# Row-by-row fetching on SyncE and ScalarE in a recommendation kernel: 245 tiles against 386

## The chip, the cores and the metric

The kernel runs on one core of one Trainium2 chip. Its time is the device time of one execution in microseconds. The kernel before took 10938.21 us (median of three runs, 10936.02 to 10938.97).

## The reference

For each of 16,384 samples, 69 user fields and one label index a table of 100,001 rows of 96 floats (384 bytes a row). An attention network gives each gathered row a weight, the weighted rows are summed by groups of fields, and a small top network follows:

```python
u = emb[batch_user]                              # 16384 x 69 x 96
q = emb[batch_label[:, 0]] broadcast over fields
z = concatenate([q, u, q - u, q * u])
h = dice(z @ W1 + b1, a1)                        # 64 wide
att = (h @ W2 + b2) @ W3 + b3                    # one weight per row
pre = where(batch_user < ITEM_NUM, u * att, 0)
pooled = einsum('gf,bfe->bge', window, pre)      # 69 fields into 10 groups
x = concatenate([pooled, ql])
h = dice(bn(x @ Wf1 + bf1), af1); h = dice(bn(h @ Wf2 + bf2), af2)
return h @ Wf3 + bf3
```

`dice(x)` is `(alpha * (1 - p) + p) * x` with `p = sigmoid(x)` after a constant scale. The arithmetic is float32.

## The kernel before, in words

The samples are cut into 32 blocks of 512. A block has 69 chunks of 512 rows each: 64 that mix eight samples with 64 fields, and 5 for the tail fields. Two chunks make a pair, and there are 1104 pairs; one **step** of the kernel is the work on one pair. A chunk is four tiles of 128 rows, so that a pair has eight tiles of 128 gathered rows.

A tile of rows comes to SBUF in one of three ways.

- Nearly all are gathered by GpSimd (POOL): one indirect DMA of 128 rows per tile (`gather`, L265, called from `fetch`, L373) into one slot of the tile `u` of the pool `upool`.
- SyncE (SP) fetches 109 tiles row by row. It issues one DMA of 384 bytes per row (L301), with the row's address taken from a register; every 32 rows it loads 32 offsets from SBUF into registers (L286).
- ScalarE (ACT) fetches 136 tiles in the same way, 16 rows in each step, between its own activations.

Tiles that SP and ACT fetch take slot 3 of a chunk and go to buffers of their own, the `ring`: four for SP and three for ACT. TensorE waits for the row count of such a tile on a semaphore (`wait_for_single`, L318) before it transposes it.

The order of the work on every engine is written out by hand: `plan` (L592) lists for each step what is recorded, and each engine runs its own instructions in that order. In step i these are, in order, the row sums of a group of four pairs (`attend_rows`, `spread`, every fourth step), `hidden(i - 2)` (four matmuls into `ph`, then two activations on ACT, L405 and L406, and a multiplication on VectorE, L407), ACT's rows of this step (`scalar_rows`, L615), `pool(i - 7)` (16 matmuls that read `u` or the ring a second time, and a copy to `pooled`), and `fetch(i)` (eight gathers or waits, eight transposes into two `ptr` tiles in PSUM, and two VectorE operations on each). What reads a tile `u` last is thus the pooling seven steps later; `upool` has 14 buffers. For each block some steps hold more: copies of a small table by ACT (`head_rows`, L342, two copies in one step), and the top network (L487 to L522) spread over ten steps, with six activations on ACT.

SP's list is short: the loads of indices and its rows. It runs ahead of the other engines until a ring buffer is not free yet.

Of the kernel before, what the change touches and what calls it, by code (L numbers as in the profile page):

```python
# [18 lines left out]
P = 128  # L19
# [29 lines left out]

ROW_BYTES = 4 * E  # L50
SLOT = 3
SP_CHUNKS = [2 * (10 * s + 8) + 1 for s in range(109)]
SP_RING = 4
ACT_CHUNKS = [2 * (8 * s + 11) for s in range(136)]
ACT_RING = 3
ACT_ROWS = 16
ACT_STEPS = -(-P // ACT_ROWS)
SINGLES = SP_CHUNKS + ACT_CHUNKS
NSB = (len(SINGLES) + P - 1) // P
NSEM = 8  # L60


def chunk_of(c):
# [52 lines left out]
def rec_kernel(  # L116
# [12 lines left out]
    nc = tc.nc  # L129
# [1 line left out]

    const = ctx.enter_context(tc.tile_pool(name="const", bufs=1))
    ipool = ctx.enter_context(tc.tile_pool(name="ipool", bufs=2))
    upool = ctx.enter_context(tc.tile_pool(name="upool", bufs=14))
    tpool = ctx.enter_context(tc.tile_pool(name="tpool", bufs=4))
    ypool = ctx.enter_context(tc.tile_pool(name="ypool", bufs=6))
    rpool = ctx.enter_context(tc.tile_pool(name="rpool", bufs=2))
# [137 lines left out]
    class Singles:  # L275

        def __init__(self, name, engine, kind, chunks, first, buffers, group):
            self.name, self.engine, self.kind, self.group = name, engine, kind, group
            self.chunks, self.first, self.buffers = chunks, first, buffers
            self.sems = [tc.alloc_semaphore(f"{name}{k}") for k in range(NSEM)]  # L280
            self.given = [0] * NSEM

# [12 lines left out]
        def fetch(self, s, start, stop):  # L295

            b, k = self.buffers[s % len(self.buffers)], s % NSEM
            for r in range(start, stop):
# [295 lines left out]
    def at(step, *work):  # L594
        plan.setdefault(step, []).extend(work)

    by_sync = Singles("sp", nc.sync, mybir.EngineType.SP, SP_CHUNKS, 0, range(SP_RING), 32)
    for s, m in enumerate(SP_CHUNKS):
        at(max(0, m // 2 - 6), lambda s=s: by_sync.fetch(s, 0, P))

    by_scalar = Singles(
        "act",
        nc.scalar,
        mybir.EngineType.Activation,
        ACT_CHUNKS,
        len(SP_CHUNKS),
        range(SP_RING, SP_RING + ACT_RING),
        2 * ACT_ROWS,
    )
    turn = {}  # L610
    for s, m in enumerate(ACT_CHUNKS):
        for k in range(ACT_STEPS):
            turn.setdefault(m // 2 - 2 - ACT_STEPS + k, []).append((s, k * ACT_ROWS, min(P, (k + 1) * ACT_ROWS)))

    def scalar_rows(i):  # L615

        for s, start, stop in turn.get(i, []):
            by_scalar.fetch(s, start, stop)

    c = NPAIR - CLOSE  # L620
    for i in range(c):
        if i >= 3 and (i - 3) % 4 == 3:
            at(i, rows_of(i - 6, 4))
        if i >= 3:
            at(i, tails_of(i - 3))
        if i >= 4 and (i - 4) % 4 == 3:
            at(i, spread_of(i - 7, 4))
        if i >= 2:
            at(i, hidden_of(i - 2))
        at(i, lambda i=i: scalar_rows(i))  # L630
        if i < c - CLOSE:
            if i >= POOL_LAG:
                at(i, pool_of(i - POOL_LAG))
        else:

            for k in {0: (-15, -14), 1: (-13,), 3: (-12, -11), 4: (-10, -9), 7: (-8, -7)}.get(i - c + 8, ()):
                at(i, pool_of(c + k))
        at(i, fetch_of(i))
# [116 lines left out]
```

## Time and profile before

| | |
|---|---|
| median of three runs | 10938.21 us |
| the profiled execution | 10926.71 us |
| its span, first to last instruction | 10924.9 us |
| mean granted TensorE clock | 0.745 |
| busy: PE / VectorE / ACT / POOL | 8862.0 / 4285.5 / 1897.5 / 8226.3 us |
| gathers on POOL, rows (L266) and labels | 8587 + 128 |
| single-row DMAs on ACT and on SP | 17408 and 13952 |
| busy share of the 16 DMA engines: gathers, ACT and SP rows | 18.7%, 0.5% and 0.4% |

All of these come from one profiled execution, except the median. The busy time of ACT does not hold its DMA issues or its register loads: they are instructions of its queue (written ACTq), and so are those of SP (SPq). An idle gap that the profile shows on ACT can therefore be filled with row issues. A wait "on issue" is time in which the engine waited for nothing that the profile shows.

### The profile page before, as it was taken

To read this page: it belongs to the slowest core of one execution; us is meant where nothing else is said; L and a number is where in the kernel's file an instruction comes from. 1 tells how busy PE (TensorE), PEld (TensorE's weight loads), DVE (VectorE), ACT (ScalarE), POOL (GpSimd) and SP (SyncE) were. 2 spreads that over 40 slices of the span, in tenths; PEclk is the share of its full clock that TensorE was granted. 3 is DMA by queue.
4 is the path that set the end of the run, shared out by engine and by line. 5 is a ranking of instruction groups with operands and counts; after the bars stand their busy time and mean duration, and the time that the engine had idled before them with its cause. 6 is when DMAs were issued, how large, how long until landed. Compare 5 with 4: busy or idle time off the path is not lost.

```text
span 10924.9 us, 172203 instructions
## 1 busy us (share of the span) xinstructions
PE 8862.0 (81%) x41797; PEld 4319.5 (40%) x41797; DVE 4285.5 (39%) x7535; ACT 1897.5 (17%) x2761; POOL 8226.3 (75%) x8721
## 2 busy tenths in 40 slices
PE   7878878788887888888878778878888887888878
PEld 3333434343333344333433333334343333433335
DVE  4334333333333333433333333333333333333334
ACT  1111111111111111111111111111111111111112
POOL 7777777777777777777777777777777777777776
PEclk7767777777777777767777777777777777777777
DMA  2212211121111212212111121112212112122111
GB/s 49 42 42 44 42 42 41 42 44 42 42 42 42 44 41 42 42 41 44 42 42 41 42 44 42 42 42 42 44 42 42 42 41 44 42 42 41 42 41 36
DMA packets 344467, 458.51 MB, mean 42 GB/s; under 512 B 202354, under 2 KB 202866, under 8 KB 343330
## 3 DMA queue, kind: packets, MB, share of 16 engines
q0 software_dynamic: 278880, 428.92, 18.7%
q1 hardware_dynamic: 29762, 11.82, 0.5%
q10 hardware_dynamic: 34816, 6.75, 0.4%
q8 instruction: 336, 5.51, 0.2%
q14 instruction: 673, 5.51, 0.2%
HBM read 446.74 MB, written 0.07 MB: 41 GB/s over the span
## 4 chain that ended last, share of the span: by engine, by line
POOL 49%; issue 21%; PE 17%; DMA 12%; DVE 0%; ACT 0%; ACTq 0%; POOLq 0%; DVEq 0%
POOL u L266 48%; DMA u<-in_rows,ids 12%; PE p L502 4%; PE acc L325 4%; PE ph L399 3%; PE ph L403 2%; PE ptr L325 2%; POOL q L266 1%; PE prow L414 1%; PE pa L423 1%; PE ph L396 0%; PE ph L401 0%; PE pc L348 0%; PE patt L431 0%; ACTq L301 0%
## 5 line engine op out<-in xcount | busy, mean ns | idle before, releaser
L266 POOL DMA_INDIRECT u<-in_rows,ids x8587 | 8104.3, 944 | 2620.1 <-issue 2428.2
L325 PE MATMUL ptr<-ident,u 128*96 128x128 f32 x8587 | 2002.8, 332 | 1940.1 <-DMA u<-in_rows,ids 1892.9
L407 DVE TENSOR_TENSOR y<-ph,y 128x512 f32<-128x512 f32 x1104 | 763.5, 692 | 4377.1 <-ACT y L406 4119.6
L325 PEld LDWEIGHTS ptr<-ident,u 128*96 128x96 f32 x8587 | 1139.7, 149 | 2701.4 <-DMA u<-in_rows,ids 2262.6
L325 PEld LDWEIGHTS acc<-rw,u 128*96 128x96 f32 x15930 | 1677.0, 187 | 1204.3 <-issue 977.6
L376 DVE COPY uT<-ptr 96x512 f32<-96x512 f32 x2208 | 1494.1, 677 | 1488.6 <-PE ptr L325 1485.2
L325 PE MATMUL acc<-rw,u 128*96 128x20 f32 x15930 | 1792.5, 258 | 57.8 <-DVE rw L436 41.7
L405 ACT ACTIVATE y<-ph 128x512 f32<-128x512 f32 x1104 | 658.6, 597 | 6308.6 <-PE ph L403 5822.7
L399 PE MATMUL ph<-uT,A 128*64 128x512 f32 x4096 | 1649.8, 883 | 0.0
L403 PE MATMUL ph<-quT,wn 96*64 96x512 f32 x4416 | 1585.2, 788 | 0.0
L379 DVE TENSOR_TENSOR quT<-ptr,qT 96x512 f32<-96x512 f32 x2048 | 1380.2, 674 | 0.0
L406 ACT ACTIVATE y<-y,wn,na1c 128x512 f32<-128x512 f32 x1104 | 898.1, 813 | 36.6
L403 PEld LDWEIGHTS ph<-quT,wn 96*64 96x64 f32 x4416 | 440.7, 188 | 1041.5 <-issue 1040.8
L502 PE MATMUL p<-pooled,wf 96*100 96x512 f32 (+1 forms) x1400 | 693.1, 644 | 0.0
L399 PEld LDWEIGHTS ph<-uT,A 128*64 128x64 f32 x4096 | 264.1, 175 | 616.2 <-issue 608.8
L416 ACT COPY row<-prow 128x512 f32<-128x512 f32 (+1 forms) x277 | 161.6, 583 | 1791.9 <-PE prow L414 1179.1
L470 DVE COPY pooled<-acc 96x160 f32<-96x160 f32 x1008 | 419.9, 417 | 117.6 <-PE acc L325 116.9
L414 PE MATMUL prow<-y,v 128*32 128x512 f32 x2208 | 453.6, 891 | 1.4 <-DVE y L407 1.1
L502 PE MATMUL p<-pre,V 96*100 96x512 f32 (+1 forms) x700 | 394.9, 710 | 3.0 <-DVE x L485 2.7
L502 PEld LDWEIGHTS p<-pooled,wf 96*100 96x100 f32 x1400 | 259.5, 198 | 332.6 <-issue 332.6
L436 DVE SCALAR_TENSOR_TENSOR rw<-patt,bb,wn 128x320 f32<-128x320 f32 x554 | 276.2, 539 | 143.6 <-PE patt L431 142.9
L431 PE MATMUL patt<-ident,row 128*128 128x128 f32 x1108 | 224.9, 340 | 25.1 <-DVE pre L424 22.7
(72 smaller groups left out, 2445.8 us busy)
## 6 DMA issues: line engine op xcount, KB each, us to landing
ring<-in_rows ACTq DMA_DIRECT2D x17408, 0.4 KB
ring<-in_rows SPq DMA_DIRECT2D x13952, 0.4 KB
u<-in_rows,ids POOLq DMA_INDIRECT x8587
ids<-in_idx SPq DMA_DIRECT2D x8, 560.0 KB, 3.9
q<-in_emb,ids POOLq DMA_INDIRECT x128
wf<-in_far SPq DMA_DIRECT2D x1, 1209.0 KB, 6.4
wn<-in_near SPq DMA_DIRECT2D x1, 236.0 KB, 2.8
ids<-in_idx SPq DMA_DIRECT2D x1, 140.0 KB, 2.3
```

The source lines that it names most:

```text
L266: nc.gpsimd.indirect_dma_start(out=dst, out_offset=None, in_=table, in_offset=bass.IndirectOffsetOnAxis(ap=index, axis=0),)
L325: ins = op(out, ring[:, at[0]].bitcast(F32) if at else u[:, 4 * (c % 2) + t, :], other, **how)
L376: nc.vector.tensor_copy(uT[j][0:E], ptr)
L379: nc.vector.tensor_tensor(quT[:, j, :].rearrange("e (s f) -> e s f", f=FM), ptr.rearrange("e (s f) -> e s f", f=FM), by_field(q[:, k * NS ...
L399: nc.tensor.matmul(p, As[n % 2][:, k // 4, :], uT[j], start=True, stop=False)
L403: nc.tensor.matmul(p, Wp, quT[:, j, :], start=False, stop=True)
L405: nc.scalar.activation(y, ph, AF.Sigmoid, scale=S_DICE)
L406: nc.scalar.activation(y, y, AF.Identity, bias=a1c, scale=na1c)
L407: nc.vector.tensor_mul(y, ph, y)
L414: nc.tensor.matmul(pr[32 * k : 32 * (k + 1), :], v2, ys[b + k], start=True, stop=True)
L470: nc.vector.tensor_copy(pooled[n][:, :, k * NS : (k + 2) * NS].rearrange("e g s -> e s g"), pa.rearrange("e j s g -> e (j s) g"),)
L502: nc.tensor.matmul(p1, w[:, h * DH : (h + 1) * DH], x, start=(k == 0), stop=(k == KTOP - 1))
```

## The change

More tiles are fetched row by row. SP fetches 199 tiles instead of 109, one per five and a half steps instead of ten, with five ring buffers instead of four. ACT fetches 187 tiles instead of 136. Its rows are now one stream, 22 in each step, that runs on from one tile to the next, so that a tile is spread over 5.8 steps instead of eight. ACT still loads 32 offsets at a time, at rows 0, 32, 64 and 96 of a tile, which is now mostly in the middle of a step's rows. The 141 tiles more are no longer gathered by POOL. `upool` has 13 buffers instead of 14. The table of offsets grows from 256 to 512 columns. The scratch size for descriptors is now written out, with the value that it had without being named.

```diff
 SLOT = 3
-SP_CHUNKS = [2 * (10 * s + 8) + 1 for s in range(109)]
-SP_RING = 4
-ACT_CHUNKS = [2 * (8 * s + 11) for s in range(136)]
+SP_CHUNKS = [2 * (int(5.5 * s) + 6) + 1 for s in range(199)]
+SP_RING = 5
+ACT_ROWS = 22
+ACT_CHUNKS = [2 * ((s + 1) * P // ACT_ROWS + 2) for s in range(187)]
 ACT_RING = 3
-ACT_ROWS = 16
-ACT_STEPS = -(-P // ACT_ROWS)
...
+RING_BYTES = 16384
...
-    upool = ctx.enter_context(tc.tile_pool(name="upool", bufs=14))
+    upool = ctx.enter_context(tc.tile_pool(name="upool", bufs=13))
...
         range(SP_RING, SP_RING + ACT_RING),
-        2 * ACT_ROWS,
+        32,
     )
-    turn = {}
-    for s, m in enumerate(ACT_CHUNKS):
-        for k in range(ACT_STEPS):
-            turn.setdefault(m // 2 - 2 - ACT_STEPS + k, []).append((s, k * ACT_ROWS, min(P, (k + 1) * ACT_ROWS)))
-
     def scalar_rows(i):
 
-        for s, start, stop in turn.get(i, []):
-            by_scalar.fetch(s, start, stop)
+        row, stop = i * ACT_ROWS, min((i + 1) * ACT_ROWS, len(ACT_CHUNKS) * P)
+        while row < stop:
+            s, start = divmod(row, P)
+            n = min(P - start, stop - row)
+            by_scalar.fetch(s, start, start + n)
+            row += n
...
-    nc = bacc.Bacc("TRN2", target_bir_lowering=False, num_devices=1)
+    nc = bacc.Bacc("TRN2", target_bir_lowering=False, num_devices=1, dynamic_dma_scratch_size=RING_BYTES)
```

## The prediction

> **What bounds the kernel now.** I read the page first: busy shares, the chain, the costliest groups.
>
> ```profile
> PE 8862.0 (81%) x41797; PEld 4319.5 (40%) x41797; DVE 4285.5 (39%) x7535; ACT 1897.5 (17%) x2761; POOL 8226.3 (75%) x8721
> ...
> POOL 49%; issue 21%; PE 17%; DMA 12%; DVE 0%; ACT 0%; ACTq 0%; POOLq 0%; DVEq 0%
> ...
> L266 POOL DMA_INDIRECT u<-in_rows,ids x8587 | 8104.3, 944 | 2620.1 <-issue 2428.2
> L325 PE MATMUL ptr<-ident,u 128*96 128x128 f32 x8587 | 2002.8, 332 | 1940.1 <-DMA u<-in_rows,ids 1892.9
> ```
>
> PE has the larger busy share, but what PE's transposes wait for is the gathers (1892.9 us), and three quarters of the chain are POOL, its issue and its DMAs. POOL looks idle for a quarter of the span, so its waits come next.
>
> ```profile
> POOL u L266 <- issue: 2428.2, 7958, 0.3
> ...
> POOL u L266 <- PE acc L325: 9.7, 32, 0.3
> ```
>
> No wait ahead of a row gather is longer than 0.3 us: the gap belongs to the gather, and POOL never waits for a buffer. The end of the timelines of POOL and VectorE shows the last gather and the last operation but a store:
>
> ```profile
> 10886.76 0.94 POOL L266 DMA_INDIRECT u<-in_rows,ids  x1 [0.30 <-issue]
> ```
> ```profile
> 10922.33 0.34 DVE L537 TENSOR_SCALAR r<-p_last,wf 1x128 f32<-1x128 f32 x1 [0.68 <-PE p_last L535]
> ```
>
> The first gather starts at 3.3 us, so 8714 intervals take 10883.5 us: 1.249 us each, and 38 us are left from the last gather's start to the end of the span. That is the whole time. A step has 1.249 x 8715 / 1104 = 9.86 us. Now ACT, in the timeline of its engine (start, length, what, idle before):
>
> ```profile
> 5019.15 0.60 ACT L405 ACTIVATE y<-ph 128x512 f32<-128x512 f32 x1 [10.71 <-PE ph L403]
> 5019.77 0.81 ACT L406 ACTIVATE y<-y,wn,na1c 128x512 f32<-128x512 f32 x1
> 5022.06 5.15 ACTq L301 DMA_DIRECT2D ring<-in_rows  x16
> 5027.31 0.60 ACT L405 ACTIVATE y<-ph 128x512 f32<-128x512 f32 x1 [6.72 <-issue]
> 5027.94 0.81 ACT L406 ACTIVATE y<-y,wn,na1c 128x512 f32<-128x512 f32 x1
> 5028.01 4.99 ACTq L301 DMA_DIRECT2D ring<-in_rows  x16
> 5033.04 1.13 ACT L349 COPY A<-pc 32x512 f32<-32x512 f32 x2 [4.29 <-PE pc L348]
> ```
>
> ACT is far busier than 17%: 16 rows fill 5 us of a step. Rows start as soon as L406 has started (5027.94, 5028.01). In the other step a register load delays them to 5022.06; the view of the load's line has it, and SP's timeline and waits follow:
>
> ```profile
> L286 ACTq TENSOR_LOAD <-offsets x544: 2132/2182/2236, 16.1 to 10735.1; - x182
> L286 SPq TENSOR_LOAD <-offsets x436: 2027/2174/2411, 4.1 to 10447.1; - x146
> ```
> ```profile
> 6.33 252.97 SPq L301 DMA_DIRECT2D ring<-in_rows  x640
> ```
> ```profile
> SPq L301 <- PE ptr L325: 3556.9, 71, 95.2
> SPq L301 <- PE acc L325: 1324.8, 26, 96.8
> ```
>
> Five tiles back to back take SP 253 us plus one load, 51.1 us a tile with four loads. It waits 4881.7 us in total for ring buffers: it is half idle.
>
> [...] from row to row (loads and the row after one left out) ACT takes 0.309 us while SP issues nothing and 0.318 us while it does. [...] the row queues take 0.5% and 0.4% of the DMA engines, the gathers 18.7%. [...] here 32 registers take 2.18 us, 68 ns each, so the trace's number is used.
>
> **The change part by part.** POOL: 141 gathers fewer (386 - 245) at 1.249 us = **-176 us**. The gather interval is 1.2494 us while SP issues and 1.2485 us while it doesn't, so denser rows cost 8574 gathers x 0.0009 us x the half of the time that is new = 4 us at most. POOL alone then gives 10926.7 - 176 = 10750.7 us for a profiled execution; the shown median lies 11.5 us above the profiled one, so 10762 us. The new step is 1.249 x 8574 / 1104 = 9.70 us.
>
> SP: 199 tiles x 51.1 = 10169 us, one per 5.5 x 9.70 = 53.4 us. It fits with 2.3 us a tile to spare; the idle half covers it. Tile 0 ends near 57 us and is needed in step 6, after some 59 gathers (77 us); the lead grows after that. The index loads in SP's list have 36 steps between their place and first use. Cost 0; without that cover (rows over 4.5% slower) TensorE would wait at each of the 199 tiles.
>
> ACT has new work, and ACT is what decides. Its queue over the 1088 steps with rows, from start times in the trace:
> - 23936 rows x 0.318 (SP nearly always issuing now) = 7612 us;
> - 748 loads x 2.47 (2.18, 0.06 to the next instruction, and the first row after a load 0.235 longer) = 1848 us;
> - 1088 x 0.70 for L405 and its semaphore (L406 runs under the rows) = 762 us;
> - 272 row copies (0.48), 93 dice pairs (1.46), 62 table copies (0.55) = 131 + 136 + 34 = 301 us.
>
> Sum 10523 us, **9.67 us a step against POOL's 9.70**. The same list for before (17408 x 0.314, 544 loads) gives 7873 us, 7.2 a step, so the 0.7 us of slack per step is really over two now. After the change it is 0.03.
>
> Behind ACT's activation wait VectorE's L407 and, in its order, the copies of the next transposes; then PE. TensorE may run one step ahead of ACT (`ph` and `ptr` have two buffers). POOL runs ahead further: today the gather into a reused `u` starts 60 us after the pooling that freed it at the median, 41 us at least. With 13 buffers it is 31 us at least. So the smaller pool costs 0 unless ACT and PE together fall 30 to 50 us behind; then POOL waits. The ACT ring (three tiles of 5.8 steps) has over two steps between last reading and rewriting; 0.
>
> What can't be hidden: once per block ACT copies the table A (L349) after its rows; PE's next row sum needs that PSUM buffer, and ACT then waits for it. I estimate 3 us x 31 = 93 us of idle from the 1.1 to 4.3 us of these gaps above (from 0 to 6 us each, so 0 to 190). ACT then ends step 1087 at 18 + 10523 + 93 = 10634 us; sixteen steps without rows at PE's 8.03 us (8862 / 1104) and 38 us of end make 10800, against 10749 from POOL. A lag under 30 us at the last row vanishes in these sixteen steps. With 1.8 us outside the span and 11.5 to the median: 10813. With half of the idle time it is 10767. I take **10795**.
>
> The extra waits of PE (141) and the longer load of offsets (64 KB more, in parallel with others at the start) are under a microsecond each in place; next to nothing.
>
> **Rivals.**
> 1. *POOL alone still sets the pace.* ACT's idle gaps are absorbed: 10750 to 10770, at 10762. For it: ACT's sum lies under POOL's. Against: by 0.3% only.
> 2. *ACT clearly the bound, still faster.* Rows at 0.322 instead of 0.318 with both queues full add 96 us: 10860 to 10915.
> 3. *Slower.* ACT's place in the loop ph, L405, L407, uT, transposes: each 0.1 us per step is 109 us. It decides from 9.89 us per step on (10960 - 11.5 - 1.8 - 38 - 128 - 18 = 10763, over 1088): 0.22 us a step more than my sum with no idle time, or rows at 0.328. SP's issuing has added 0.009 already; as much again and the idle time would do it. At 0.335 it would be 11127 even without idle time. Against: half of ACT's rows ran beside SP's already.
> 4. *The change doesn't do what it says*, its SP tiles coming late because its rate falls short: at 0.345 a row, a tile takes 53 us. SP's rows are 0.330 whether ACT issues or not, so it is unlikely; inside 3.
>
> **How the numbers follow.** ACT and POOL about level, 10770 to 10860: 0.48. Rival 1: 0.24. Rival 2: 0.10. Within 0.2% (which is about what a measurement of this kernel can tell from no change; 10916 to 10960): 0.05. Slower: 0.13. So faster 0.82. The range 10750 to 10920 leaves out the last two cases and little below. All the likely cases have one sign.
>
> **What would show it.** The gathers 8446, their interval 1.249 us between waits, ACT's waits for ph near zero in total (5822.7 us now), SP's ring waits under 600 us. Right: POOL's waits for PE at L266 between 0 and 100 us in sum. Rival 1: none, and PE still waiting for gathers as long as now. Rivals 2 and 3: POOL waiting for acc for hundreds of us, ACT solid with rows and loads. Wrong: if rows or loads lengthen with both queues full, or ACT idles at the A copies or dice of each block by over 6 us.

## The result and the profile after

The changed kernel takes 11046.32 us (median of four runs, 11035.63 to 11064.66) against 10937.11 us before: the ratio is 1.0102, with a 95% interval of 1.0089 to 1.0115. It is 109 us slower; 10795 us was forecast. The profiled execution took 11064.66 us, its span 11062.9 us.

The page of the changed kernel answers to the first lines of the prediction: busy time, the chain that ended last, and the same two groups.

```profile
PE 8420.5 (76%) x41797; PEld 4332.3 (39%) x41797; DVE 4172.0 (38%) x7535; ACT 1872.5 (17%) x2761; POOL 8102.7 (73%) x8580
...
ACTq 56%; issue 14%; PE 14%; ACT 8%; DMA 4%; POOL 3%; DVE 2%; POOLq 0%; DVEq 0%
...
L266 POOL DMA_INDIRECT u<-in_rows,ids x8446 | 7980.5, 945 | 2837.2 <-issue 2361.7
...
L325 PE MATMUL ptr<-ident,u 128*96 128x128 f32 x8446 | 1544.5, 327 | 407.8 <-issue 193.9
```

The 141 gathers are gone, and ACT is busy for 17% as before. The chain has changed hands: POOL had 49% of it and now has 3%, and ACT's queue, which had none, has 56%. TensorE's transposes waited 1892.9 us for gathers; now it is 163.8 us. POOL's waits, and the end of POOL's and of VectorE's timeline in the changed kernel:

```profile
POOL u L266 <- issue: 2361.7, 7700, 2.1
POOL u L266 <- PE ptr L325: 215.9, 202, 7.9
...
POOL u L266 <- PE acc L325: 75.2, 50, 7.0
```
```profile
10981.16 0.94 POOL L266 DMA_INDIRECT u<-in_rows,ids  x1 [0.30 <-issue]
```
```profile
11060.28 0.34 DVE L537 TENSOR_SCALAR r<-p_last,wf 1x128 f32<-1x128 f32 x1 [0.68 <-PE p_last L535]
```

POOL now waits for buffers, up to 7.9 us at a time, and ends 82 us before the span does, where it was 38. It runs ahead and is held back. ACT's timeline in the changed kernel shows by what (start, length, what, idle before):

```profile
5046.86 0.60 ACT L405 ACTIVATE y<-ph 128x512 f32<-128x512 f32 x1 [6.53 <-issue]
5047.49 0.81 ACT L406 ACTIVATE y<-y,wn,na1c 128x512 f32<-128x512 f32 x1
5047.56 9.65 ACTq L301 DMA_DIRECT2D ring<-in_rows  x22
5057.25 0.60 ACT L405 ACTIVATE y<-ph 128x512 f32<-128x512 f32 x1 [8.95 <-PE ph L403]
5057.88 0.81 ACT L406 ACTIVATE y<-y,wn,na1c 128x512 f32<-128x512 f32 x1
5057.95 9.76 ACTq L301 DMA_DIRECT2D ring<-in_rows  x22
5067.76 0.60 ACT L405 ACTIVATE y<-ph 128x512 f32<-128x512 f32 x1 [9.06 <-issue]
```

There is no gap in this stretch: each activation starts some 0.1 us or less after the end of the rows ahead of it. The "idle" of 9 us that the profile gives before an activation is filled with rows, and the releaser that it names (PE, at 5057.25) had been done for 5.1 us. A step with a register load in its rows takes 10.4 us from activation to activation, more than POOL's 9.70.

The loads and SP's waits for ring buffers in the changed kernel:

```profile
L286 ACTq TENSOR_LOAD <-offsets x748: 2129/2292/2500, 17.2 to 10873.2; - x187
```
```profile
SPq L301 <- PE ptr L325: 444.0, 92, 16.0
SPq L301 <- PE acc L325: 119.0, 17, 20.4
```

A load on ACT now takes 2.29 us at the median where it took 2.18. SP still waits 563 us for buffers, so SP is not what is late.

From the start times in the trace, ACT's queue between its first row (19.4 us) and its last (10886.0 us) is made of the following. A wait is what an interval ahead of an activation or a copy has beyond the median of its kind; after a table copy it is what goes beyond the 0.60 us of those that did not wait.

| | forecast | measured |
|---|---|---|
| 23936 rows, the longer ones after loads included | 7788 | 7792 |
| 748 register loads | 1672 | 1756 |
| activations and copies | 1063 | 1053 |
| sum without waits | 10523 | 10601 |
| ACT's waits for other engines | 93 | 266 |
| in all, us | 10616 | 10867 |

With 19 us before and 177 us after that is the span. The sum without waits, 9.74 us for each of the 1088 steps, is already over POOL's 9.70; with the waits it is 9.99.

### The profile page after: what moved, and what is told of

Read it like the earlier page. It is cut to its first block, busy times and chain, and to the rows that moved or that the text cites. A ratio compares the mean times of both kernels' runs of the same rounds, so it can differ in the third digit from the quotient of the medians.

```text
span 11062.9 us, 208859 instructions
## 1 busy us (share of the span) xinstructions
PE 8420.5 (76%) x41797; PEld 4332.3 (39%) x41797; DVE 4172.0 (38%) x7535; ACT 1872.5 (17%) x2761; POOL 8102.7 (73%) x8580
## 4 chain that ended last, share of the span: by engine, by line
ACTq 56%; issue 14%; PE 14%; ACT 8%; DMA 4%; POOL 3%; DVE 2%; POOLq 0%; DVEq 0%
ACTq L301 44%; ACTq L286 12%; ACT y L405 5%; DMA u<-in_rows,ids 4%; POOL u L266 3%; PE acc L325 2%; PE p L502 2%; PE ph L403 2%; PE ph L399 2%; PE ptr L325 1%; ACT y L406 1%; PE prow L414 1%; PE pa L423 1%; PE ph L396 1%; PE ph L401 1%
## 5 line engine op out<-in xcount | busy, mean ns | idle before, releaser
L266 POOL DMA_INDIRECT u<-in_rows,ids x8446 | 7980.5, 945 | 2837.2 <-issue 2361.7
L325 PE MATMUL ptr<-ident,u 128*96 128x128 f32 x8446 | 1544.5, 327 | 407.8 <-issue 193.9
L399 PE MATMUL ph<-uT,A 128*64 128x512 f32 x4096 | 1510.3, 811 | 0.0
L403 PE MATMUL ph<-quT,wn 96*64 96x512 f32 x4416 | 1412.6, 708 | 0.0
L414 PE MATMUL prow<-y,v 128*32 128x512 f32 x2208 | 744.8, 858 | 673.7 <-DVE y L407 569.6
L403 PEld LDWEIGHTS ph<-quT,wn 96*64 96x64 f32 x4416 | 407.4, 174 | 933.7 <-issue 933.0
L502 PE MATMUL p<-pooled,wf 96*100 96x512 f32 (+1 forms) x1400 | 613.5, 581 | 0.0
L414 PEld LDWEIGHTS prow<-y,v 128*32 128x32 f32 x2208 | 83.3, 127 | 1063.0 <-DVE y L407 838.6
L502 PEld LDWEIGHTS p<-pooled,wf 96*100 96x100 f32 x1400 | 232.0, 178 | 281.7 <-issue 281.6
```

Source lines behind the costliest of these rows:

```text
L266: nc.gpsimd.indirect_dma_start(out=dst, out_offset=None, in_=table, in_offset=bass.IndirectOffsetOnAxis(ap=index, axis=0),)
L325: ins = op(out, ring[:, at[0]].bitcast(F32) if at else u[:, 4 * (c % 2) + t, :], other, **how)
L399: nc.tensor.matmul(p, As[n % 2][:, k // 4, :], uT[j], start=True, stop=False)
L403: nc.tensor.matmul(p, Wp, quT[:, j, :], start=False, stop=True)
L414: nc.tensor.matmul(pr[32 * k : 32 * (k + 1), :], v2, ys[b + k], start=True, stop=True)
L502: nc.tensor.matmul(p1, w[:, h * DH : (h + 1) * DH], x, start=(k == 0), stop=(k == KTOP - 1))
```

## The experiments

Theory A: ScalarE's queue is overfull, and nothing else is dearer. Rival B: the denser rows, the smaller pool or the ring slow the other engines. All edits are to the changed kernel unless the text says otherwise.

**On other chips.** The first five runs fell on two chips where the kernel before took 13737 and 13794 us, so none of their numbers can be set beside 11046 us. They are SyncE's part alone, ScalarE's part alone, 20 rows, the copies on VectorE, and 20 rows once more; their edits are shown further down with the runs that repeated them.

> SyncE's part of the change alone (199 tiles, five ring buffers, 13 buffers of u), ScalarE as before (136 tiles, 16 rows a step). Theory A, ScalarE's queue sets the pace after the change and nothing else is dearer: 8497 gathers, 90 fewer at 1.249 us, so 10938 - 112 = 10826 us, no wait of POOL. Rival B, the denser single rows, the 13 buffers or the ring slow the others: above 10880 us, with waits of POOL or PE that the kernel before doesn't have.

> ScalarE's part alone (187 tiles, 22 rows a step), SyncE as before (109 tiles). Theory A: ScalarE's queue is still full; its rows get back about 0.005 us each where SyncE is idle (23936 x 0.005 = 115 us), so near 10930 us, POOL's own floor being 10938 - 51 x 1.249 = 10874 us. Rival B, two full queues in each other's way are the cause: near the floor, 10874 us, or below 10890 us.

> The changed kernel with 20 rows in a step on ScalarE instead of 22 (170 tiles instead of 187). Theory A: ScalarE loses 2176 rows x 0.319 and 68 loads x 2.35 us = 854 us of queue, falls far under POOL, and POOL sets the time: 8463 gathers, 10938 - 124 x 1.249 = 10783 us. Rival B (SyncE's density, the smaller pool or ring): stays above 10950 us.

> The changed kernel with the copies of L416 (row sums, 277) and L349 (table A, 64) moved from ScalarE to VectorE. Theory A: 131 + 34 us leave ScalarE's queue, and with them its waits for TensorE around these copies (some 50 to 130 us): 11046 less 215 to 295, so 10750 to 10830 us, POOL's floor being 10762. Rival B or a bound by waits elsewhere in the loop: 11000 us or more.

> The changed kernel with 20 rows in a step on ScalarE instead of 22 (170 tiles instead of 187). The first look at it fell on a chip where the kernel before takes 13737 us too, with single rows that are slower there; this asks again. Theory A, ScalarE's queue is what the change overfilled: 2176 rows x 0.319 and 68 loads x 2.35 us = 854 us leave it, it falls far under POOL, and POOL sets the time: 8463 gathers, 10938 - 124 x 1.249 = 10783 us. Rival B, SyncE's density, the smaller pool or the ring hold the others up: above 10950 us.

Measured: 16568, 15016, 16689 and 16682 us on the first chip, 16748 us on the second. All miss theory A's numbers; that four of them lie in rival B's open bands tells nothing on chips where the kernel before takes a quarter more. Four have SyncE's 25472 rows and end within 180 us of each other, whatever ScalarE does; ScalarE's part alone, the 15016 us, has ScalarE's queue on 56% of its chain. The chain of the four, here of SyncE's part alone, and the view of the line that issues rows say why:

```profile
SPq 62%; issue 36%; PE 1%; another core or an unknown queue 0%; DMA 0%; DVE 0%; ACT 0%; POOL 0%; ACTq 0%
```
```profile
L301 SPq MOVE ring<-in_rows x25472: 1/29/1491, 6.6 to 16468.1; - x199
L301 SPq DMA_DIRECT2D ring<-in_rows x25472: 1/228/1434, 6.7 to 16468.2; - x199
```

The median instruction is as long as ever, but some take up to 1.5 us, and a row with its share of loads costs SyncE 0.65 us: in these four runs SyncE was the bound. Why its instructions stall there stays open. The runs below were made later, on chips where the kernel before took 10927 to 10942 us.

**The copies moved off ScalarE.**

```diff
-            nc.scalar.copy(As[n % 2][E:P, ...], pc[E:P])
+            nc.vector.tensor_copy(As[n % 2][E:P, ...], pc[E:P])
...
-        nc.scalar.copy(row, pr)
+        nc.vector.tensor_copy(row, pr)
```

> The changed kernel with the copies of L416 and L349 on VectorE instead of ScalarE, asked again because the first look fell on a chip where all kernels ran a quarter slower. Theory A, ScalarE's queue is overfull: 165 us leave it, and some 50 to 130 us of its waits around these copies: 10750 to 10830 us against 10938 before. Rival B, the loop's other waits or the density of rows: 11000 us or more.

Measured: 10883.42 us against 10926.56 before, ratio 0.9960 (0.9944 to 0.9976). That is 163 us less than the changed kernel as the medians stand, and 152 where each is taken from its own kernel before; 165 us of work were taken from ScalarE's queue, and from its first row to its last it takes 168 us less in the trace. VectorE, which got the work, has 2% of the chain. That speaks for A. But the run misses both bands: it ends over the 10830 us of A and over POOL's floor. ScalarE's queue has 41% of the chain now, and POOL and the gathers' DMAs, which had 3% and 4%, have 12% each:

```profile
ACTq 41%; issue 14%; PE 13%; POOL 12%; DMA 12%; ACT 6%; DVE 2%; POOLq 0%
```

**20 rows a step.**

```diff
-ACT_ROWS = 22
-ACT_CHUNKS = [2 * ((s + 1) * P // ACT_ROWS + 2) for s in range(187)]
+ACT_ROWS = 20
+ACT_CHUNKS = [2 * ((s + 1) * P // ACT_ROWS + 2) for s in range(170)]
```

> The changed kernel with 20 rows a step on ScalarE (170 tiles). Theory A, ScalarE's queue was overfull at 22: 854 us leave it, it falls under POOL, and POOL sets the time: 8463 gathers, before less 124 x 1.249 = 155 us, about 10775 to 10785 us. Rival B, SyncE's density, 13 buffers or the ring: above 10900 us.

Measured: 10777.35 us against 10926.58, ratio 0.9863 (0.9834 to 0.9891), as theory A has it. The kernel with 17 tiles *more* on POOL is 269 us faster than the changed one (258 with each taken from its own kernel before). POOL has the chain again, and its waits are back to 0.3 us:

```profile
POOL 40%; PE 23%; issue 18%; DMA 12%; ACTq 5%; ACT 1%; DVE 1%; POOLq 0%; DVEq 0%
```
```profile
POOL u L266 <- issue: 2382.9, 7806, 0.3
POOL u L266 <- DMA u<-in_rows,ids: 88.5, 290, 0.3
```

SyncE's 199 tiles, the ring of five and the 13 buffers are all in this kernel, so none of them costs that time by itself.

**Each part alone.** SyncE's part on the kernel before (`SP_CHUNKS`, `SP_RING` and 13 buffers, ScalarE with 136 tiles), and ScalarE's part with SyncE's 109 tiles:

> SyncE's part alone (199 tiles, ring of five, 13 buffers), ScalarE as before. Theory A: POOL sets the time with 8497 gathers, before less 90 x 1.249 = 112 us, about 10815 to 10826 us, and POOL waits for nobody. Rival B: above 10880 us.

> ScalarE's part alone (187 tiles at 22 rows), SyncE as before. Theory A: ScalarE's queue is full, its rows a little cheaper where SyncE idles (up to 115 us): 10930 to 11046 us. Rival B, two full queues in each other's way are what costs: under 10890 us, POOL's floor being 10874.

Measured against 10926.58: SyncE's part alone 10817.83 us, ratio 0.9900 (0.9871 to 0.9929), the 109 us that 90 gathers are worth. ScalarE's part alone 10921.99 us, ratio 0.9997 (0.9989 to 1.0004), 8 us under the band of theory A and far over that of rival B: 51 gathers fewer and no gain, since ScalarE's queue is the chain there too.

```profile
ACTq 57%; PE 15%; issue 14%; ACT 8%; POOL 2%; DVE 2%; DMA 1%; POOLq 0%
```

Together they take 11046: that is 124 us over ScalarE's part alone, 114 with each taken from its own kernel before. In the trace some 110 us of it are ScalarE's rows, 0.3141 us each where SyncE is half idle and 0.3188 where it isn't; why they take longer there isn't shown.

**No register loads on ScalarE.**

```diff
         def load(self, s, start):
 
+            if self.kind == mybir.EngineType.Activation and hasattr(self, "kept"):
+                self.values = dict(enumerate(self.kept, start))
+                return
             i, stop = self.first + s, min(P, start + self.group)
...
             self.values = dict(enumerate(values, start))
+            self.kept = values
```

> The changed kernel with ScalarE's register loads left out after the first: ScalarE fetches the same 32 rows again and again (so its rows are the wrong ones, in the same number). Theory A: 747 x 2.35 = 1756 us leave ScalarE's queue, and POOL's own pace shows: 8446 gathers, before less 141 x 1.249 = 176 us, about 10750 to 10762 us. Rival B: above 10900 us.

Measured: 10869.67 us against 10926.58, ratio 0.9941 (0.9918 to 0.9964). It lies between the two: under the 10900 us of rival B, and 108 us over the 10762 of theory A. ScalarE's queue, with 1% of the chain, is no longer what is late; POOL has the chain (41%), and TensorE waits for gathers about as long as before (1800.0 us). POOL's waits in this run:

```profile
POOL u L266 <- issue: 2394.3, 7745, 2.1
POOL u L266 <- DMA u<-in_rows,ids: 204.3, 471, 1.8
```

Waits of up to 2.1 us where no buffer is missing: a stretch of POOL's timeline shows the gap of 0.30 us growing for some gathers.

```profile
1470.54 0.94 POOL L266 DMA_INDIRECT u<-in_rows,ids  x1 [0.31 <-issue]
...
1473.12 0.94 POOL L266 DMA_INDIRECT u<-in_rows,ids  x1 [0.39 <-DMA u<-in_rows,ids]
1474.55 0.94 POOL L266 DMA_INDIRECT u<-in_rows,ids  x1 [0.48 <-DMA u<-in_rows,ids]
1476.17 0.94 POOL L266 DMA_INDIRECT u<-in_rows,ids  x1 [0.68 <-DMA u<-in_rows,ids]
```

Over the run, 260 gaps are longer than 0.36 us; what they have beyond the usual 0.305 is 109 us in all, and that is the missing time. The run with the copies on VectorE has 262 such gaps with 117 us, the one with 20 rows none. So I formed theory C: beyond some rate of single rows (4.62 per us in this run, 4.46 in the one with 20 rows) POOL is held. The pages' queue lines, of the run with 20 rows and then of this one, have the packets' time, as a share of 16 engines. q0 is POOL's gathers, q1 SyncE's queue and q10 ScalarE's, as their counts tell: with two packets a row, 2 x 21760 is 43520. (So the 0.5% and 0.4% in the table of the kernel before belong to SyncE and ScalarE in this order.)

```profile
q0 software_dynamic: 274912, 422.81, 19.0%
q1 hardware_dynamic: 52802, 16.36, 1.1%
q10 hardware_dynamic: 43520, 8.44, 0.7%
```
```profile
q0 software_dynamic: 274368, 421.98, 20.6%
q1 hardware_dynamic: 52802, 16.42, 2.6%
q10 hardware_dynamic: 47872, 9.29, 2.1%
```

With 4.6% more rows, the packets of SyncE's and ScalarE's rows take 2.6 times as long in sum; the median packet of 384 bytes takes 174 ns instead of 22. Rival D: it is ScalarE's 22 rows a step, or the repeated rows of this run. The repeated rows can be left out at once: the run with the copies on VectorE repeats none and has the same gaps.

**The same with fewer tiles on SyncE, and 21 rows.** To the kernel without loads:

```diff
-SP_CHUNKS = [2 * (int(5.5 * s) + 6) + 1 for s in range(199)]
+SP_CHUNKS = [2 * (6 * s + 6) + 1 for s in range(183)]
```

> The kernel without ScalarE's register loads (ScalarE fetches wrong rows, in the same number), with a tile per six steps on SyncE (183 tiles instead of 199): 47360 single rows instead of 49408, 8462 gathers instead of 8446. Theory C, the rate of single rows holds POOL: 4.4 rows per us, no held gathers, before less 125 x 1.249: 10770 us, 100 us faster although POOL gathers 16 tiles more. Rival D, ScalarE's 22 rows a step or the repeated rows hold POOL: 10870 us and more, 20 us slower by the added gathers.

To the changed kernel, `ACT_ROWS = 21` and 178 tiles; the same with the copies on VectorE; and the changed kernel as it is:

> The changed kernel with 21 rows a step on ScalarE (178 tiles, 48256 single rows). Theory A, ScalarE's queue: 0.41 us a step leave it against 22 rows, so it needs about 9.55 of POOL's 9.71 us a step and POOL sets the time, 8455 gathers, 132 fewer: 10926.6 - 165 = 10762 us. Theory C (added after the run without register loads stayed at 10870 us): over some 4.4 single rows per us [...] gathers land late and POOL is held; at 4.5 rows per us part of the 109 us of held gathers shows: 10775 to 10850 us. Rival B: above 10900 us.

> 21 rows a step on ScalarE and the copies of L416 and L349 on VectorE. Theory A alone: 10762 us, POOL's floor with 8455 gathers, as with 21 rows and the copies on ScalarE. Theory C: as that run, 10775 to 10850 us, and not faster than it by more than 20 us, since the copies don't change the rate of single rows.

> The changed kernel as it is, beside the others on one chip: 11035 to 11065 us as shown before. Theory A: ScalarE's queue without a gap; theory C: on top of it, packets of 384 bytes slow and POOL held at times.

Measured against 10941.83: without loads and with fewer SyncE tiles 10800.59 us, ratio 0.9874 (0.9845 to 0.9902). POOL has 16 gathers more and the kernel is faster, by 69 us as it stands and by 84 us where each is taken from its own kernel before. Theory C is right on the sign, and rival D, which expected 10870 us or more, is not the main cause; taken from the same kernel before, 15 us over C's number remain. 21 rows: 10782.98 us, ratio 0.9857 (0.9829 to 0.9886); with the copies moved as well 10782.31 us, ratio 0.9857 (0.9828 to 0.9885), no difference. That lies in the band of theory C, but also within 6 us of POOL's floor by theory A (10941.83 less 165), so these two runs do not tell A from C. The changed kernel: 11046.29 us, ratio 1.0098 (1.0069 to 1.0128), as shown before.

Set out by the rate of single rows between the first and the last of them, from the traces. The 384-byte packets are of two kinds, about 22 ns and about 175 ns long, with few between (in the changed kernel the medians of the two are 22 and 182), so the table has the share of the long ones:

| run | rows per us | 384-byte packets over 100 ns | gaps of POOL over 0.36 us: number, us in all |
|---|---|---|---|
| before | 2.92 | 4% | 0, 0 |
| SyncE's part alone | 4.03 | 5% | 0, 0 |
| 20 rows | 4.46 | 12% | 0, 0 |
| no loads, fewer SyncE tiles | 4.46 | 34% | 43, 21 |
| 21 rows | 4.56 | 35% | 11, 4 |
| 22 rows, copies on VectorE | 4.62 | 52% | 262, 117 |
| 22 rows, no loads | 4.62 | 57% | 260, 109 |

The share grows with the rate, with no edge to be seen in it; POOL's lost time is small up to 4.56 rows per us and over 100 us at 4.62. The mean rate is not all, though. At 4.46 rows per us the run with 20 rows has 12% of long packets and no longer gap, and the run without loads has 34% and 43, whose 21 us are about what remained over C's number. How the rows follow each other within a step may be the difference, which would be a part of rival D; no run tests that.

The changed kernel itself has 4.54 rows per us, because ScalarE's queue slows it, and 30% of long packets. Of its POOL's 206 gaps over 0.36 us, 109, with 44 of 259 us, wait for no engine that the profile names: they look like those of the runs above, and the others are the waits for buffers shown with the result. In its chain POOL has 3% and DMA 4%.

Why POOL is held isn't shown. A row is two packets in the trace, one of 384 bytes and one of 4, and a gather is sixteen of 3072 bytes and sixteen of 4; the traces don't tell the DMA engines apart. What they show is that the packets of both kinds take longer: without loads those of the gathers, 0.2% fewer, take 9% longer in sum than with 20 rows (20.6% of 10867.9 us against 19.0% of 10775.4), beside the 2.6 times of the rows' packets. That this is what holds POOL is my estimate, not tested, and what POOL waits for then is open too: no run changed the scratch for descriptors.

## Why the prediction was wrong, point by point

- *What bounds the kernel now*: right. SyncE's part alone gave the time of its gathers, 109 us where 112 were worked out, and so did 20 rows.
- *SP fits*: right; it waited 563 us for ring buffers, under the 600 of the forecast.
- *ACT's rows*: right to 4 us of 7788 in sum, 0.3188 us from row to row with both queues full.
- *"748 loads x 2.47"*: mis-sized by 84 us. Ahead of the change a load always followed an activation and took 2.174 us. Of the 748 loads, 680 now stand behind a row and take 2.296; the 67 behind an activation still take 2.174. The section on the change says that loads move into the middle of the rows, and the price was taken from loads that weren't there.
- *"What can't be hidden"*: this is the term that failed most. It had 93 us of idle time at the table copies, of which the point of 10795 took about 75 (all of it gives 10813, half 10767). ScalarE waited 266 us. The mechanism is there, some 48 us at these copies; the rest lies at places that the sum did not have: 112 us at activations right behind rows, 87 us between a row-sum copy and its activation, 19 us mostly at the top network. TensorE and ScalarE wait for each other in turns, and with no slack each such wait stays in the sum. The sum was put at 10800 us to the end of the span; it is 11063. Of these 263 us, 173 are waits and 84 are loads.
- *From level to slower*: the sum without waits came out at 9.74 us a step, not 9.67, 0.7% over, because of the loads. Against a margin of 0.3% that alone decided which engine is the bound; the waits then came on top and made it slower than before. Rival 3 had the place and the price right (0.1 us a step is 109 us), and its point, 9.89 us a step, was passed: 10867 / 1088 is 9.99. It was given 0.13, and the range left it out. With two sums 0.3% apart, and one of them made of several priced terms, of which the loads came out 5% dearer, that chance was far too small.
- *"POOL: -176 us ... 4 us at most" for denser rows*: wrong as well, though hidden in the shown result. The gather interval was compared with SP on and off, in a kernel with 2.9 rows per us. At 4.62 POOL loses some 110 us (run without loads), 62% of the gain. In the changed kernel itself it did not set the time.
- *Buffers, ring, 13 instead of 14*: right; all are in the 20-row kernel, which runs at POOL's pace. POOL's longer waits for PE in the changed kernel fit ScalarE's lag, in the order the prediction gave. The table of offsets grew by 128 KB (128 to 256 in the traces), not by 64; its one load takes 2.7 us instead of 2.2, next to nothing as said.

The better kernels are those with 20 or 21 rows, 10777 and 10783 us, 1.4% under the kernel before on the same chips.

## What to carry to other kernels

When work moves from a full engine to another one's queue, add up that queue per step, waits included, and leave it a margin of several per cent: with 21 rows a step, its sum without waits 4% under POOL's, this kernel was 1.4% faster than before; with 22, 0.4% over, it was 1% slower. ACT's busy share, 17% before and after, doesn't show its queue; start times do. Price an instruction at the place where it will stand (a load took 2.296 us behind a row and 2.174 behind an activation), and POOL's gathers at the rate of single rows that they will meet (no gap over 0.36 us at 2.92 per us, 109 to 117 us in such gaps at 4.62).

## What was not expected

- A register load of 32 values on ScalarE takes 2.296 us behind a row and 2.174 us behind an activation.
- With more single rows of 384 bytes per us in two queues, more of their packets take about 175 ns instead of 22: 12% at 4.46 (20 rows), 35% at 4.56, over half at 4.62, where POOL's gathers lose over 100 us in gaps that the kernel before doesn't have.
- A row on ScalarE takes 1.5% longer where SyncE issues nearly all the time than where it is half idle (0.3141 to 0.3188 us).
- On two chips the kernel before took a quarter more time; in the trace of SyncE's part alone on one of them, single-row fetches stalled, some for up to 1.5 us, so often that SyncE needed 0.65 us a row.
